# Talking-heads attention in a decoder kernel: a written order on every engine, and an entry's steps over six ticks

## The chip, the cores and the metric

The kernel runs on one core of a Trainium2 chip. The core has four engines that compute, each with an instruction queue of its own that is worked off in order: PE (TensorE, matrix products), DVE (VectorE), ACT (ScalarE) and POOL (GpSimd). SP (SyncE) issues most of the transfers (DMAs) between the chip's main memory and the on-chip memory. The metric is the device time of one execution in microseconds (us); lower is better. The times of before are a median of three executions, and one more execution was recorded by the hardware profiler.

## What is computed

The reference is a decoder of four blocks of attention, cross attention and feed-forward on x of 32 entries x 128 tokens x 128 features. The change lies in one stage, the talking-heads attention of the last block (`_L3_attn_ref`), here cut to what matters, for 16 heads of 64 features:

```python
q, k, v = (x @ Wq, x @ Wk, x @ Wv)                  # split into heads; 4 memory columns go ahead of k and v
q, k = l2norm(q), l2norm(k)
dots = einsum('bhid,bhjd->bhij', q, k) * 10.0       # 128 x 132 for each head
dots = einsum('hg,bgij->bhij', W_pre_th, dots)      # mix the heads
dots = where(causal, -max, dots)
vk = top_k(dots, 64)[0][..., -1:]                   # the 64th largest of each row
attn = softmax(where(dots < vk, -max, dots))
attn = einsum('hg,bgij->bhij', W_post_th, attn)     # mix the heads again
out = einsum('bhij,bhjd->bhid', attn, v) * head_scale_params
out = out * sigmoid(x @ Wg + bg)
return out @ Wo
```

x here is the layer-normed input, and the result is added to x.

## The kernel before, in words

The kernel runs the twelve layers one after the other, each as a stage of its own. The stage in question is `l3_attn` of class `Fast` (from line 2079). Its loop goes over ticks; each tick calls seven functions, each for another of the 32 entries, so that the steps of one entry are spread over five ticks: `queries` at lag 0, `dots` and `mixed` at lag 1, `ranked` and `kept` at lag 2, `spread` (with `gates` for every second entry) at lag 3, `outputs` at lag 4. `normed` prepares four entries at a time.

One entry goes this way:

- `queries`: PE multiplies x by the weights of q and k (into the pool p2); ACT squares each half (tile sq) and copies it (tile raw); DVE sums the squares (ss, line 2173) and makes the first guess of the reciprocal root (`rsqrt`, lines 1784 and 1785); POOL refines it in twelve small operations (lines 1787 to 1791) and scales raw (line 2176).
- `dots`: PE transposes raw (line 2188), ACT copies the transposes to qT and kT, PE multiplies them head by head (dp), ACT copies the products (tile dots, line 2197). SP writes them to main memory in 16 DMAs (scr, line 2204) and reads them back in one, with head and row inside the partition (tile rows, line 2207).
- `mixed`: PE mixes the heads and adds the causal mask (mp); ACT makes the exponentials (ex, line 2224) and a plain copy (e2, line 2225; the profile calls it e); POOL subtracts a middle part of e2 from a mask (neg, line 2228), so that the same instructions can find smallest values there.
- `ranked`: DVE searches the 64th largest value of each row. The rows stand in 16 blocks `ib` of 8 query positions; blocks 0 to 6 need no search. A round is MAX8 (the eight largest) and MATCH_REPLACE8 (strike them out), which comes with a MATCH_VALUE_LOAD. Blocks 14 and 15 are searched in e2 with eight MAX8 each (lines 2241 and 2243), blocks 7 to 13 in neg with one to seven (lines 2253 and 2255). Lines 2258 and 2259 pick the thresholds (sel, thr).
- `kept`: DVE strikes out what is under the threshold and sums the rest (line 2270, an operation of two inputs, with an accumulator read), and takes reciprocals (den, line 2272); POOL multiplies ex by them in eight operations (line 2277). The `with` at line 2273 puts these behind the neg of the next entry on POOL.
- `spread`: PE mixes again (am for the four memory columns, tp for the rest); ACT copies (am, aT); POOL spreads am over a block-diagonal tile (aM, line 2289); PE and ACT make v.
- `outputs`: PE multiplies by v (op), DVE multiplies by the gates (o, line 2330), PE projects (y), DVE adds to X (`addx`, line 387) and takes the statistics of the next norm (lines 360 and 361).

All matrix products that are issued through a helper carry line 355 in the profile; the tile's name tells them apart. Two kinds of on-chip accumulator banks are used by all steps: p2 (two buffers) and p1 (four).

What sets the order: in this stage the framework's scheduler is free. It takes all instructions, with their dependencies, and lays each engine's queue by priority and by its own estimate of durations; the order of the text is only where it begins. Two other stages (`stream` and `l3_ffn`) use the class `Ordered` (line 1347) instead: it wraps each engine in a `Lane` (line 1329), which ties every instruction to the one traced before it on that engine, so that the queue follows the text. DMAs issued by SP are not in a lane.

Of the kernel before, what the change touches and what calls it, by code (L numbers as in the profile page):

```python
# [1358 lines left out]
class Fast(General):  # L1359
# [417 lines left out]
    def rsqrt(self, wk, v, name, eng=None):  # L1777

        nc, n = self.nc, v.shape[-1]
        eng = eng or nc.vector  # L1780
        y = wk.tile([128, n], F32, tag="ry" + name, name="ry")
        t = wk.tile([128, n], F32, tag="rt" + name, name="rt")
        yi = y.bitcast(I32)
        nc.vector.tensor_scalar(yi, v.bitcast(I32), 1, None, ALU.logical_shift_right)
        nc.vector.tensor_scalar(yi, yi, -1.0, 1597463007.0, ALU.mult, ALU.add)
        for _ in range(3):
            eng.tensor_tensor(t, y, y, ALU.mult)
            if eng is nc.gpsimd:
                eng.tensor_tensor(t, t, v, ALU.mult)
                eng.tensor_scalar(t, t, -0.5, 1.5, ALU.mult, ALU.add)  # L1790
                eng.tensor_tensor(y, t, y, ALU.mult)
            else:
                eng.scalar_tensor_tensor(t, t, -0.5, v, ALU.mult, ALU.mult)
                eng.scalar_tensor_tensor(y, t, 1.5, y, ALU.add, ALU.mult)
        return y
# [283 lines left out]
    def l3_attn(self):  # L2079
        if self.general:  # L2080
            return super().l3_attn()
        nc, tc, i = self.nc, self.tc, self.i
        J, WID, AT, PAT = 132, self.WID, self.AT, self.PAT
        with ExitStack() as es:
# [77 lines left out]
            def queries(n):  # L2162
                x = X[n // 4][:, 128 * (n % 4):128 * (n % 4) + 128]
                raw = wk.tile([128, 32, 64], F32, tag="raw", name="raw")
                ss = wk.tile([128, 32], F32, tag="ss", name="ss")
                for w in range(2):
                    pp = self.p2([128, 16, 64], "qk")
                    for u in range(2):
                        self.mm(pp[:, 8 * u:8 * u + 8, :], x, aw[:, w, 512 * u:512 * u + 512])
                    sq = wk.tile([128, 16, 64], F32, tag="sq", name="sq")  # L2170
                    nc.scalar.activation(sq, pp, AF.Square)
                    nc.scalar.copy(raw[:, 16 * w:16 * w + 16, :], pp)
                    nc.vector.tensor_reduce(ss[:, 16 * w:16 * w + 16], sq, AX.X, ALU.add)
                nc.vector.tensor_scalar(ss, ss, 1e-24, None, ALU.max)
                rn = self.rsqrt(wk, ss, "s", nc.gpsimd)
                nc.gpsimd.tensor_tensor(raw, raw, rn.unsqueeze(2).to_broadcast([128, 32, 64]), ALU.mult)
                S[n] = {"raw": raw}

            def dots(n):
                flat = S[n]["raw"].rearrange("p h d -> p (h d)")  # L2180
                qT = wk.tile([128, 8, 128], F32, tag="qT", name="qT", bufs=1)
                kT = kT2[n % 2]
                for w, dst in ((0, qT), (1, kT[:, :, 4:J])):
                    for u in range(2):
                        p = self.p1([128, 4, 128])
                        for c in range(4):
                            o = 1024 * w + 512 * u + 128 * c
                            nc.tensor.transpose(p[:, c, :], flat[:, o:o + 128], self.ident)
                        nc.scalar.copy(dst[:, 4 * u:4 * u + 4, :], p)
                d = wk.tile([128, 8, 2, J], F32, tag="dots", name="dots", bufs=1)  # L2190
# [19 lines left out]
            def mixed(n):  # L2210
# [4 lines left out]
                for u, parts in enumerate((((0, 0, 416), (416, 0, 400)), ((816, 0, 264), (1080, 0, 264)))):  # L2215
                    p = self.p2([128, 2, 512], "mp")
                    for v, (at, _, m) in enumerate(parts):
                        w = 416 if u == 0 else 264
                        h = (416 * v if u == 0 else 832 + 264 * v)
                        self.mm(p[:, v, 0:w], self.identh[:, 0, :], hide[:, h:h + w], stop=False)  # L2220
                        self.mm(p[:, v, 0:m], mix1, rows[:, at:at + m], start=False)
                    w = 416 if u == 0 else 264
                    dst = slice(0, 832) if u == 0 else slice(832, 1360)
                    nc.scalar.activation(ex[:, dst].rearrange("p (v j) -> p v j", v=2), p[:, :, 0:w], AF.Exp)
                    nc.scalar.copy(e2[:, dst].rearrange("p (v j) -> p v j", v=2), p[:, :, 0:w])

                neg = wk.tile([128, 748], F32, tag="neg", name="neg")
                turn = nc.gpsimd.tensor_tensor(neg, hide2, e2[:, 348:1096], ALU.subtract)
                s.update(e2=e2, ex=ex, neg=neg, turn=turn)

            def ranked(n):

                s = S[n]
                t16 = t16_2[n % 2]
                top = wk.tile([128, 2, 8], F32, tag="top", name="top")
                thr = wk.tile([128, 7], F32, tag="thr", name="thr")
                for ib in (14, 15):
                    cur = seg(s["e2"], ib, 0, 8 * ib + 12)
                    work = wk.tile([128, J], F32, tag="work", name="work", bufs=1)
                    for r in range(8):  # L2240
                        nc.vector.max(top[:, ib - 14, :], cur)
                        if r < 7:
                            nc.vector.match_replace(out=work[:, 0:8 * ib + 12], in_to_replace=top[:, ib - 14, :],  # L2243
                                                    in_values=cur, imm_value=-3.4e38)
                            cur = work[:, 0:8 * ib + 12]
                for ib in range(7, 14):
# [13 lines left out]
                s.update(thr=thr, top=top)  # L2260

            def kept(n):
# [10 lines left out]
                with tc.issue_after(S[n + 1]["turn"].ins) if n + 1 < NB else ExitStack():  # L2273
                    for q in range(4):
                        for o, lo, m in ((exm2[n % 2][:, 4 * q:4 * q + 4, 0:4], 0, 4),
                                         (four(ex, q, 4, WID[q] - 4), 4, WID[q] - 4)):
                            nc.gpsimd.tensor_tensor(o, four(ex, q, lo, m),
                                                    d[:, 4 * q:4 * q + 4].unsqueeze(2).to_broadcast([128, 4, m]), ALU.mult)

            def spread(n):  # L2280
# [7 lines left out]
                aM = wk.tile([128, 16, 16, 8], F32, tag="aM", name="aM", bufs=1)  # L2288
# [8 lines left out]
                v = wk.tile([128, 1024], F32, tag="v", name="v")  # L2297
# [5 lines left out]
                s.update(aM=aM, v=v)  # L2303
# [15 lines left out]
            def outputs(n):  # L2319
                s = S.pop(n)  # L2320
# [8 lines left out]
                o = wk.tile([128, 8, 128], F32, tag="o", name="o", bufs=1)  # L2329
                nc.vector.scalar_tensor_tensor(o, T[n // 2][:, :, 128 * (n % 2):128 * (n % 2) + 128], 1.0, op,  # L2330
                                               ALU.add, ALU.mult)
                y = self.p1([128, 128], "y")
                for c in range(8):
                    self.mm(y, o[:, c, :], awo[:, c, :], start=c == 0, stop=c == 7)
                self.addx(n, y)

            T = {}
            normed(0)
            for t in range(NB + 5):
                if t % 4 == 3 and t + 1 < NB:  # L2340
                    normed((t + 1) // 4)
                for fn, lag in ((dots, 1), (queries, 0), (outputs, 4), (spread, 3), (ranked, 2), (mixed, 1), (kept, 2)):
                    n = t - lag
                    if 0 <= n < NB:
                        if fn is spread and n % 2 == 0:
                            gates(n // 2)
                        fn(n)
            self.look(den)

# [567 lines left out]
```

## Time and profile before

| | us |
|---|---|
| median of three executions | 6465.49 (6462.71 to 6470.9) |
| the profiled execution's own time | 6466.63 |
| its span, first to last instruction | 6464.7 |
| busy in the span: PE / DVE / POOL / ACT | 5634.8 / 4862.1 / 3699.6 / 3286.9 |
| first matmul of the stage on its weights (tile aw) | starts at 1855.5 |
| first and last neg (entries 0 and 31) | 1901.4 and 2810.0 |
| last addition to X in the stage | starts at 2850.36 |

The profile gives busy time per engine, groups of instructions by line, engine and tile with their mean durations and the idle time before them, what each wait ended on, and the instructions in order of time. In such lines `out<-in` are the tiles written and read, followed by partitions x elements. A duration runs from an instruction's start to its end, and on DVE two independent instructions may overlap a little: the start of the next one, not the end of the last, tells how long an instruction holds its engine. The times within the profile count from the start of the span.

### The profile page before, as it was taken

Reading aid. Unit: us, or ns where it says so; the run is one execution under the profiler, and the core shown is the slowest. Engines: PE = TensorE matmul, PEld = TensorE weight load, DVE = VectorE, ACT = ScalarE, POOL = GpSimd, SP = SyncE. Lnnn points to the kernel's source line nnn. Section 1 sums busy time; section 2 is a strip of 40 time slices with the busy share of each in tenths; the row PEclk is TensorE's granted clock in tenths of the full one; section 3 lists DMA queues with packets and bytes.
Section 4 is the critical chain, followed back from the end, with each engine's and each line's share of the span. In section 5 each row is a group of like instructions: output and inputs, shape, how many; then the busy total and the mean of one; then the engine's idle time right before and its main releaser. Section 6 shows DMA issues by size and latency. Waiting matters only on the chain.

```text
span 6464.7 us, 137972 instructions
## 1 busy us (share of the span) xinstructions
PE 5634.8 (87%) x56460; PEld 3993.0 (62%) x56705; DVE 4862.1 (75%) x11852; ACT 3286.9 (51%) x4413; POOL 3699.6 (57%) x4504
## 2 busy tenths in 40 slices
PE   7955966776868888876999999999999999999998
PEld 4533546664556666664676666667767666766765
DVE  4566533335549998866889988989998998998985
ACT  4645631113535555532556655665655665566554
POOL 0031001011015555523888888888888888888885
PEclk9977977668989999987999999999999999999999
DMA  1000037543002121210000000000000000000000
GB/s 40 2 1 1 2 143 237 176 138 98 8 20 51 46 50 45 51 32 34 1 1 1 14 5 1 14 5 1 1 14 5 1 14 5 1 1 1 1 1 15
DMA packets 243267, 207.49 MB, mean 32 GB/s; under 512 B 125651, under 2 KB 230458, under 8 KB 237503
## 3 DMA queue, kind: packets, MB, share of 16 engines
q1 hardware_dynamic: 239020, 161.73, 8.7%
q0 software_dynamic: 2304, 33.56, 1.4%
q8 instruction: 448, 7.34, 0.5%
q10 hardware_dynamic: 1298, 3.26, 0.1%
q14 instruction: 197, 1.61, 0.1%
HBM read 140.57 MB, written 57.93 MB: 31 GB/s over the span
## 4 chain that ended last, share of the span: by engine, by line
PE 51%; DVE 16%; POOL 2%; ACT 2%; issue 2%; DMA 0%; POOLq 0%; DVEq 0%; ACTq 0%
PE qk L1342 9%; PE sc L1342 6%; PE av L1342 6%; PE y L1342 5%; PE rT L1342 4%; PE vp L1342 4%; DVE raw L1342 2%; PE ap L1342 2%; PE gp L1342 2%; PE fy L1342 2%; PE oTp L1342 2%; PE y L355 2%; DVE ry L1342 2%; DVE work L2243 1%; PE tp L355 1%
## 5 line engine op out<-in xcount | busy, mean ns | idle before, releaser
L1342 POOL TENSOR_TENSOR raw<-raw,rt 128x1024 f32<-128x1024 f32 x384 | 1035.2, 2709 | 37.4 <-DVE raw L1342 37.4
L1342 POOL TENSOR_TENSOR raw<-raw,ry 128x2048 f32<-128x2048 f32 x192 | 741.4, 3861 | 15.0
L1342 PE MATMUL qk<-wqkv,zs 128*128 128x512 f32 x1536 | 730.0, 598 | 6.3 <-DVE zs L1342 6.3
L1342 DVE TENSOR_TENSOR raw<-qk,tab 128x1024 f32<-128x1024 f32 x384 | 700.3, 1824 | 1.3
L1342 ACT COPY qk<-qk 128x1024 f32<-128x1024 f32 x384 | 388.7, 1012 | 398.9 <-PE qk L1342 398.9
L1342 DVE TENSOR_TENSOR rt<-qk,tab 128x1024 f32<-128x1024 f32 x384 | 499.1, 1300 | 103.9 <-POOL ry L1342 44.4
L1342 PE MATMUL rT<-ident,raw 128*128 128x128 f32 x3072 | 431.2, 279 | 86.4 <-DVE qkT L1342 59.6
L1342 PEld LDWEIGHTS rT<-ident,raw 128*128 128x128 f32 x3072 | 345.3, 142 | 233.1 <-issue 99.8
L1342 ACT COPY va<-vp 128x1024 f32<-128x1024 f32 (+1 forms) x232 | 218.4, 942 | 506.6 <-PE vp L1342 505.2
L1342 DVE TENSOR_REDUCE ss<-sq 128x16 f32<-128x1024 f32 x384 | 462.8, 1205 | 0.0
L1342 ACT ACTIVATE PT<-sc 128x1024 f32<-128x1024 f32 x384 | 372.7, 1025 | 168.9 <-PE sc L1342 168.4
L1342 ACT ACTIVATE sq<-qk 128x1024 f32<-128x1024 f32 x384 | 407.9, 1062 | 75.3 <-DVE ss L1342 67.5
L1342 PEld LDWEIGHTS y<-wo,oT 128*128 128x128 f32 x3072 | 372.9, 192 | 91.1 <-issue 89.3
L1342 PEld LDWEIGHTS sc<-qkT 64*128 64x128 f32 x6144 | 359.0, 188 | 81.8 <-issue 81.8
L1342 PE MATMUL av<-va,P 128*64 128x65 f32 x12288 | 400.7, 223 | 0.0
L1342 ACT ACTIVATE P<-sc 128x1024 f32<-128x1024 f32 x384 | 372.5, 1022 | 51.3 <-PE sc L1342 50.2
L1342 PE MATMUL sc<-qkT 64*128 64x128 f32 x6144 | 395.8, 279 | 0.0
L1342 PEld LDWEIGHTS av<-va,P 128*64 128x64 f32 x12288 | 374.1, 137 | 23.8 <-issue 0.8
L1342 PEld LDWEIGHTS qk<-wqkv,zs 128*128 128x128 f32 x1536 | 264.9, 192 | 196.7 <-issue 189.1
L1342 POOL TENSOR_TENSOR X<-X,brep 128x512 f32<-128x512 f32 x24 | 30.5, 1272 | 617.8 <-DVE xn L1342 617.8
L1342 PE MATMUL y<-wo,oT 128*128 128x128 f32 x3072 | 374.3, 275 | 0.8 <-DVE qkT L1342 0.8
L1342 PE MATMUL vp<-wqkv,zs 128*128 128x512 f32 x768 | 361.6, 593 | 0.0
(438 smaller groups left out, 13099.8 us busy)
## 6 DMA issues: line engine op xcount, KB each, us to landing
rows<-scr SPq DMA_DIRECT2D x32, 672.0 KB
tup<-whole SPq DMA_DIRECT2D x8, 2048.0 KB
gt<-tup SPq DMA_DIRECT2D x64, 256.0 KB
tdn<-whole SPq DMA_DIRECT2D x8, 2048.0 KB
gd<-tdn SPq DMA_DIRECT2D x128, 128.0 KB
T<-flt SPq DMA_DIRECT2D x16, 1024.0 KB
wqkv<-in_dqkv SPq DMA_DIRECT2D x6, 1536.0 KB
scr<-dots SPq DMA_DIRECT2D x128, 66.0 KB
```

Of the source, the lines that this page charges most:

```text
L355: self.nc.tensor.matmul(out, lhsT=lhsT, rhs=rhs, start=start, stop=stop)
L1342: self.last = call(*a, **k)
L2243: nc.vector.match_replace(out=work[:, 0:8 * ib + 12], in_to_replace=top[:, ib - 14, :], in_values=cur, imm_value=-3.4e38)
```

## The change

`l3_attn` now runs under `Ordered`: on PE, DVE, ACT and POOL every instruction keeps the place that the text gives it. The functions are cut into smaller ones so that the text can be laid out: `queries` is called for q and for k separately, `summed` takes the sums and the guess, `scaled` POOL's part, `turned` the transposes; `ranked` becomes `ranked_above` (blocks 14 and 15) and `ranked_below` (7 to 13), their loops unchanged; neg moves to `negated`, POOL's multiplications by den to `divided` (the four small ones now ahead of the four large), v and the gates to `valued`; `outputs` becomes `weighted`, `gated`, `outputs` and `added`. `rsqrt` gets its first guess from a function `guess` of its own, with the same two instructions. The explicit tie of line 2273 goes. The lags grow by one behind `mixed`: an entry now takes six ticks. `normed` comes at the end of its tick, not at the start. No instruction is added or left out.

```diff
-    def rsqrt(self, wk, v, name, eng=None):
...
+    def guess(self, wk, v, name):
+        nc = self.nc
+        y = wk.tile([128, v.shape[-1]], F32, tag="ry" + name, name="ry")
         yi = y.bitcast(I32)
         nc.vector.tensor_scalar(yi, v.bitcast(I32), 1, None, ALU.logical_shift_right)
         nc.vector.tensor_scalar(yi, yi, -1.0, 1597463007.0, ALU.mult, ALU.add)
+        return y
+
+    def rsqrt(self, wk, v, name, eng=None, y=None):
...
+        y = self.guess(wk, v, name) if y is None else y
...
     def l3_attn(self):
...
-        nc, tc, i = self.nc, self.tc, self.i
+        tc, i, plain = self.tc, self.i, self.nc
+        nc = self.nc = Ordered(plain, tc)
...
-            def queries(n):
+            def queries(n, w):
...
+                pp = self.p2([128, 16, 64], "qk")
+                for u in range(2):
+                    self.mm(pp[:, 8 * u:8 * u + 8, :], x, aw[:, w, 512 * u:512 * u + 512])
+                sq = wk.tile([128, 16, 64], F32, tag="sq", name="sq")
+                nc.scalar.activation(sq, pp, AF.Square)
+                nc.scalar.copy(S[n]["raw"][:, 16 * w:16 * w + 16, :], pp)
+                S[n]["sq"].append(sq)
+
+            def summed(n):
+                ss = S[n]["ss"]
+                for w, sq in enumerate(S[n]["sq"]):
                     nc.vector.tensor_reduce(ss[:, 16 * w:16 * w + 16], sq, AX.X, ALU.add)
                 nc.vector.tensor_scalar(ss, ss, 1e-24, None, ALU.max)
-                rn = self.rsqrt(wk, ss, "s", nc.gpsimd)
+                S[n]["y0"] = self.guess(wk, ss, "s")
+
+            def scaled(n):
+                raw = S[n]["raw"]
+                rn = self.rsqrt(wk, S[n]["ss"], "s", nc.gpsimd, S[n]["y0"])
                 nc.gpsimd.tensor_tensor(raw, raw, rn.unsqueeze(2).to_broadcast([128, 32, 64]), ALU.mult)
...
-                neg = wk.tile([128, 748], F32, tag="neg", name="neg")
-                turn = nc.gpsimd.tensor_tensor(neg, hide2, e2[:, 348:1096], ALU.subtract)
...
+            def negated(n):
+
+                neg = S[n]["neg"] = wk.tile([128, 748], F32, tag="neg", name="neg")
+                nc.gpsimd.tensor_tensor(neg, hide2, S[n]["e2"][:, 348:1096], ALU.subtract)
...
+            def ranked_above(n):
                 s = S[n]
...
                 for ib in (14, 15):
...
+            def ranked_below(n):
+                s = S[n]
...
                 for ib in range(7, 14):
...
-                with tc.issue_after(S[n + 1]["turn"].ins) if n + 1 < NB else ExitStack():
-                    for q in range(4):
...
+            def divided(n):
+                ex, d = S[n]["ex"], den[:, n, :]
+                parts = [(exm2[n % 2][:, 4 * q:4 * q + 4, 0:4], q, 0, 4) for q in range(4)]
+                parts += [(four(ex, q, 4, WID[q] - 4), q, 4, WID[q] - 4) for q in range(4)]
+                for o, q, lo, m in parts:
+                    nc.gpsimd.tensor_tensor(o, four(ex, q, lo, m),
+                                            d[:, 4 * q:4 * q + 4].unsqueeze(2).to_broadcast([128, 4, m]), ALU.mult)
...
+            steps = ((ranked_above, 3), (mixed, 2), (weighted, 5), (gated, 5), (ranked_below, 3), (scaled, 1), (turned, 1),
+                     (queries, 0, 0), (dots, 1), (kept, 3), (divided, 4), (spread, 4), (negated, 2), (outputs, 5),
+                     (queries, 0, 1), (summed, 0), (added, 5), (valued, 4))
             for t in range(NB + 5):
+                for fn, lag, *a in steps:
+                    if 0 <= t - lag < NB:
+                        fn(t - lag, *a)
                 if t % 4 == 3 and t + 1 < NB:
                     normed((t + 1) // 4)
-                for fn, lag in ((dots, 1), (queries, 0), (outputs, 4), (spread, 3), (ranked, 2), (mixed, 1), (kept, 2)):
-                    n = t - lag
-                    if 0 <= n < NB:
-                        if fn is spread and n % 2 == 0:
-                            gates(n // 2)
-                        fn(n)
             self.look(den)
+        self.nc = plain
```

The pairs in `steps` are a function and its lag; a third number is the half that `queries` makes.

## The prediction

> **What bounds the kernel now.** I read the page's slices first (VectorE, the DVE row, is at 8 to 9 tenths from slice 11 to 17), then found the stage by its tiles: the first matmul on aw starts at 1855.5 us, the last write of X by line 387 ends at 2850.65. The subtractions into neg, one per entry, run from 1901.4 to 2810.0: 31 steps, 29.31 us each. The table of stretches gives the shares inside the stage (columns: stretch, length, then busy us of PE, PEld, DVE, ACT, POOL).
>
> ```profile
> core 0: us, PE busy (x) PEld busy (x) DVE busy (x) ACT busy (x) POOL busy (x), PEclk, DMA share, GB/s
> 2300.00:2700.00 400.00, 345.52 (x2628) 259.28 (x2626) 358.62 (x1970) 215.32 (x343) 207.95 (x302) 0.96 0.19 46
> ```
>
> 400 us hold 13.65 entries. Per entry DVE is busy 26.3 us of 29.3, PE 25.3, ACT 15.8, POOL 15.2. DVE is the bound, PE close behind. The groups of DVE by form say that not all of DVE's time is work.
>
> ```profile
> L2241 DVE MAX8 top<-work 128x8 f32<-128x132 f32 x91 | 25.9, 284 | 0.0
> L2258 DVE TENSOR_TENSOR sel<-t,pick 128x112 f32<-128x112 f32 x14 | 9.8, 698 | 0.4
> L2270 DVE SCALAR_TENSOR_TENSOR ex<-e,top,ex 128x132 f32<-128x132 f32 x14 | 14.5, 1036 | 0.0
> L2270 DVE SCALAR_TENSOR_TENSOR ex<-e,thr,ex 128x68 f32<-128x68 f32 x14 | 10.2, 729 | 0.4
> ```
>
> The third row has a median of 340 ns and a longest of 3623: now and then it stands still as long as a POOL operation (aM takes 3722). With the 124-wide sister (873 against 323) the excess per entry is 0.70 + 0.55 + 0.46 + 0.44 = 2.15 us. MAX8 shows none. So DVE's real work is 26.3 - 2.15 = **24.1 us**; 2.15 are stalls beside POOL, 3.0 idle. The waits in the same stretch (total us, times, longest) name most of that idle time:
>
> ```profile
> DVE top L2241 <- ACT e L2225: 15.1, 13, 1.2
> DVE t L2253 <- POOL neg L2228: 10.0, 13, 0.8
> ```
>
> The first is 1.1 us per entry: ranking waits for e2 of the same tick; the second is 0.73.
>
> Last I looked at how the ranking runs. Columns: start, duration, instruction. First a stretch of two independent blocks in turn, then the end of the last block, alone.
>
> ```profile
> 2827.36 0.45 DVE L2253 MAX8 t<-neg 128x8 f32<-128x116 f32 x2
> 2827.72 0.08 DVE L2255 MATCH_VALUE_LOAD neg<-t,neg 128x8 f32 x1
> 2827.78 0.27 DVE L2255 MATCH_REPLACE8 neg<-t,neg 128x116 f32<-128x116 f32 x1
> 2827.96 0.09 DVE L2255 MATCH_VALUE_LOAD neg<-t,neg 128x8 f32 x1
> 2828.03 0.26 DVE L2255 MATCH_REPLACE8 neg<-t,neg 128x108 f32<-128x108 f32 x1
> 2828.20 0.45 DVE L2253 MAX8 t<-neg 128x8 f32<-128x116 f32 x2
> ```
>
> ```profile
> 2831.20 0.09 DVE L2255 MATCH_VALUE_LOAD neg<-t,neg 128x8 f32 x1
> 2831.28 0.27 DVE L2255 MATCH_REPLACE8 neg<-t,neg 128x116 f32<-128x116 f32 x1
> 2831.58 0.28 DVE L2253 MAX8 t<-neg 128x8 f32<-128x116 f32 x1
> 2831.90 0.27 DVE L2258 TENSOR_TENSOR sel<-t,pick 128x112 f32<-128x112 f32 x1
> 2832.20 0.27 DVE L2259 TENSOR_REDUCE thr<-sel 128x7 f32<-128x112 f32 x1
> ```
>
> In the first, two rounds (MAX8, load, replace) take 0.84 us, 0.42 each, because the next instruction starts before the previous ends: the replace of 0.27 is followed after 0.18. In the second each instruction needs the one before, and starts 0.30 to 0.32 after it, its duration plus 0.03 to 0.04. **A dependent start costs 0.12 us more than an independent one** (0.30 - 0.18; for 132 columns 0.284 + 0.035 - 0.20 = 0.12; for 76 columns 0.22 + 0.035 - 0.14 = 0.115).
>
> **The change, part by part.** Nothing is added or removed in work; only neg's POOL edge goes, and the queues of PE, DVE, ACT and POOL now follow the text. SP's 17 DMAs per entry stay; no DMA is issued elsewhere in the loop.
>
> *DVE.* Before, the scheduler was free to mix blocks; the trace shows blocks of ib 14 and 15 running in turn with those of 7 to 13. Now ranked_above and ranked_below are written block by block, round by round, so MAX8, load, replace, MAX8 is one dependent chain. Rounds with a replace per entry: 2 x 7 above, 0+1+...+6 = 21 below, 35 in all. Each has two dependent starts (load after MAX8, MAX8 after replace; the load hides 0.06 before its replace in both orders). 35 x 2 x 0.12 = 8.4 us. Nine more chains are written end to end (sel, thr, first kept, reciprocal, maximum of ss, two of the guess, two of added): 9 x 0.11 = 1.0 us. Against this the stalls (2.15) and waits go: the two-input operations stand in kept, after ranking. The tick of DVE becomes 24.1 + 8.4 + 1.0 = **33.5 us**. Replace to MAX8 is in the trace; MAX8 followed at once by its own load is not. Its price lies between 0 (the load starts as after a stranger, then the tick is 33.5 - 35 x 0.12 = 29.3) and 0.15 (one gap more than sel shows; 34.6). I take 0.12 by the nearest row, sel after MAX8, 0.32 for a duration of 0.28.
>
> The Trainium skill, page "VectorE: DVE Perf Modes", section "The DRAIN you can't avoid", holds against this: after every operation the next waits until the pipe is empty, and leaving out semaphores between chained copies saves nothing. By that, dependent order would be free, DVE's tick 24.1 and the time that of the faster rival below. The rows above disagree (0.18 against 0.30), and I go by them.
>
> *POOL.* Per tick from 2502 to 2525: small rsqrt steps 3.9, raw 3.6, divided 3.5, aM 3.7, neg 1.8, 16.5 us. Counting from the start of ranked_above, scaled begins at -0.7 (its guess is done before added and normed), raw ends at 6.9, divided at 10.4; aM waits for PE's am behind dots (about 14) and ends near 18, neg near 20. kept starts at 10.1 + 1.1 + 15.3 = 26.5: cover of 6 us; if it goes, kept stalls as now, up to 2.15 us.
>
> *PE and ACT.* mixed 2.7 and weighted 3.6 stand first, turned after raw (6.9), queries, dots; am and tp to about 18, y, queries, v, gates to 24 (29 with gates). gated on DVE comes at 10.1 and needs weighted, done by about 3.5 to 7: cover of 3 us or more. Behind a late gated stand ranked_below and all of DVE; PE's dots too, if they need op's bank (two banks of that pool). summed comes at 29.4, its sq is there near 24; added comes at 32, y near 20. All these cost nothing while DVE's tick is 33.5.
>
> *Loop through the DMAs.* turned(n), queries, dots(n), rows(n), mixed(n), weighted, turned(n+1) are now a closed chain in PE's order. PE's parts: 1.75 + 1.85 + 2.6 + 2.7 + 3.6, plus a last copy of 0.7. The DMA leg:
>
> ```profile
> 2553.90 8.28 SPq L2204 DMA_DIRECT2D scr<-dots  x16
> 2564.73 0.34 SPq L2207 DMA_DIRECT2D rows<-scr  x1
> ```
>
> DMA traffic ceases at 2568.5, so the leg takes at least 14.6 us; for the first entry mixed started 7.4 after the issue, so at most 18.3. The loop is 27.8 to 31.5: under 33.5, but no faster than today's 29.3 by more than 1.5.
>
> *Sum.* 31 steps of 33.5 against 29.31: +130. Ticks 3, 4 lack gated and added (1.8 each), ticks 32, 33 lack summed (2.9 each), a little of it eaten by the loop: -8. Fill: ranking of entry 0 now stands behind summed(2), whose queries stand behind mixed(0), which waits for rows (1894 to 1897); 1897 + mixed 1.5, turned 1.9, queries and dots 7, sq 1, reduce and guess 1.9 is 1910, against 1901.4: +9. Drain: from ranking of entry 31, 29.4 + the 15.5 that today's tail takes after the reciprocal (2835.5 to 2851.2), against 41.2: +4. Sum +135. The profiled execution took 6466.63 us (span 6464.7 and 1.9 around it), the median is 1.1 less: 6601.8 and 6600.6. I say **6601**.
>
> **Rivals.**
>
> *Faster: dependent starts are free.* If a chain costs DVE nothing, its tick is 24.1, and PE, 25.3 busy, sets a tick near 26: 31 x -3.3 + 13 = -89, 6376. For it: DVE's 5.1 us of stalls and waits do go. Against: the 0.30 rows, and the DMA loop of at least 27.8. Break-even with today is a tick near 28.9, or 0.05 per dependent start instead of 0.12. Chance 0.04.
>
> *Half the price.* MAX8 to load costs nothing: DVE's tick is 29.3, and the DMA loop (27.8 to 31.5, middle 29.7) decides: 31 x 0.4 + 13 = +25, about 6490. Chance 0.07.
>
> *In-order queues wait for each other.* Dots are held by op's bank until gated (11.2), then go singly through one bank (+3), and rows, mixed and weighted miss the next gated. The slack on that path is about 5 us for an ordinary tick; the tick with gates and normed has less. Ticks of 34.7 to 36.5: 6640 to 6695. For: 16 instructions in four queues share two banks. Against: each order above has slack. Chance 0.07.
>
> *The order isn't kept, DVE still mixes blocks.* Then stalls go and waits stay, 6450 to 6480, in the middle 6465. Against: every instruction traced in the stage is tied to its predecessor. Chance 0.02.
>
> **How the numbers follow.** Forecast 0.80: its own span is the price of a dependent start, 0.11 to 0.13 (1.6 us per tick, 50 us), so 6576 to 6626, and ends 10 us uncertain. The range 6560 to 6640 adds the near edge of the queue rival and leaves out the half price and the faster cases. A measurement can tell 0.2%, 12.9 us, from no change. Slower: 0.80 + 0.07 + 0.07 = 0.94, less 0.02 for a half price that falls inside 0.2%: 0.92. Faster 0.04 + 0.01, same 0.02 + 0.01.
>
> **What would show it.** Right: one entry every 33 to 34 us, DVE above 95% busy or waiting only on itself; MAX8 of block 15 starting 0.30 to 0.32 after the replace before it and loads 0.3 after their MAX8; the form ex<-e,top,ex 128x132 at 340 ns with no 3.6 us case; POOL idle while kept runs. Wrong: loads 0.2 after their MAX8; DVE waiting for PE op or PE y every tick; PE waiting for rows at mixed and late at turned.

## The result, and the profile after

| | before | after |
|---|---|---|
| median of the compared executions, us | 6468.19 (6462.71 to 6473.0) | 6625.66 (6620.1 to 6648.61) |
| ratio, with its 95% interval | 1 | 1.025 (1.0225 to 1.0276) |
| span of the profiled execution, us | 6464.7 | 6621.9 |
| start of the last entry's addition to X, us | 2850.36 | 3012.69 |

The changed kernel is slower by 2.5%, 157.5 us by the medians. The end of the stage moved by 162.3 us; what comes after the stage takes 5.1 us less, which makes the 157.2 us of the spans. So all of it is in this stage.

The table of stretches of the kernel after, for the same 400 us as before (columns: stretch, length, then busy us of PE, PEld, DVE, ACT, POOL, the granted clock, DMA share, GB/s):

```profile
2300.00:2700.00 400.00, 306.53 (x2251) 223.62 (x2250) 367.13 (x1719) 183.36 (x293) 177.86 (x268) 0.91 0.18 42
```

DVE is busy for more of the time than before (367.1 against 358.6) and starts fewer instructions (1719 against 1970). PE, ACT and POOL all do less in the same time. An engine that is busier and gets less done has longer instructions, or instructions that overlap less. The groups by form tell which (in the last two columns: total us and mean ns of one, then idle us before them):

```profile
L1342 DVE MAX8 top<-work 128x8 f32<-128x132 f32 x77 | 23.0, 299 | 2.7
...
L1342 DVE SCALAR_TENSOR_TENSOR ex<-e,top,ex 128x132 f32<-128x132 f32 x12 | 4.2, 352 | 0.0
L1342 DVE SCALAR_TENSOR_TENSOR ex<-e,thr,ex 128x68 f32<-128x68 f32 x12 | 3.4, 280 | 0.0
L1342 DVE TENSOR_TENSOR sel<-t,pick 128x112 f32<-128x112 f32 x12 | 3.3, 274 | 0.4
```

The two-input operations, which took 1036, 729 and 698 ns before, take 352, 280 and 274: the stalls beside POOL are gone. MAX8 itself went from 284 to 299. The time is between the instructions. Here are two rounds of block 14 of the kernel after, in order of time (start, duration):

```profile
2526.29 0.29 DVE L1342 MAX8 top<-work 128x8 f32<-128x124 f32 x1
2526.61 0.09 DVE L1342 MATCH_VALUE_LOAD work<-top,work 128x8 f32 x1
2526.69 0.27 DVE L1342 MATCH_REPLACE8 work<-top,work 128x124 f32<-128x124 f32 x1
2526.99 0.29 DVE L1342 MAX8 top<-work 128x8 f32<-128x124 f32 x1
2527.32 0.09 DVE L1342 MATCH_VALUE_LOAD work<-top,work 128x8 f32 x1
```

Read the first column. From MAX8 to its load 0.32 to 0.33 us, from the replace to the next MAX8 0.30: each starts when the one before has ended, and 0.03 later. A round takes 0.70 to 0.71 us (0.725 with 132 columns, 0.695 with 116). Before, two rounds in turn took 0.84 in the rows with 116 and 108 columns.

The waits in the same stretch (total us, times, longest) show that no other engine holds DVE up; the only one of DVE's with a place in the list is the last row, and PE waits for the DMAs but has room for it:

```profile
POOL rt L1342 <- DVE ry L1342: 139.3, 12, 12.5
...
PE mp L1342 <- DMA rows<-scr: 31.4, 9, 6.1
...
DVE xnT L1342 <- PE p L1342: 1.7, 3, 0.6
```

On the chips of the experiments below the kernel before itself took between 6448 and 6668 us (once 18040), and in six of the profiles (runs 4 to 7, 9 and 10) the part behind the stage takes 3699 to 3795 us instead of the 3609 to 3642 of the others; therefore the experiments are read mainly by lengths inside the stage, beside the program's times, whose medians take slow executions in and whose ratios leave them out.

### The profile page after: what moved, and what is told of

The parts are those of the page before. It is cut to its first block, busy times and chain, and to the rows that moved or that the text cites. A ratio compares the mean times of both kernels' runs of the same rounds, so it can differ in the third digit from the quotient of the medians.

```text
span 6621.9 us, 138235 instructions
## 1 busy us (share of the span) xinstructions
PE 5682.8 (86%) x56705; PEld 4000.9 (60%) x56705; DVE 5017.2 (76%) x11852; ACT 3282.7 (50%) x4413; POOL 3699.5 (56%) x4504
## 5 line engine op out<-in xcount | busy, mean ns | idle before, releaser
L1342 POOL TENSOR_TENSOR raw<-raw,ry 128x2048 f32<-128x2048 f32 x224 | 857.5, 3828 | 17.6
L1342 POOL TENSOR_TENSOR rt<-ry 128x32 f32<-128x32 f32 (+1 forms) x816 | 235.3, 288 | 633.5 <-DVE ry L1342 526.8
L1342 ACT ACTIVATE sq<-qk 128x1024 f32<-128x1024 f32 x448 | 473.3, 1057 | 202.8 <-PE qk L1342 125.7
L1342 DVE TENSOR_REDUCE ss<-sq 128x16 f32<-128x1024 f32 x448 | 536.5, 1203 | 48.4 <-ACT sq L1342 48.4
L1342 POOL TENSOR_SCALAR rt<-rt 128x32 f32<-128x32 f32 (+1 forms) x816 | 343.6, 421 | 71.4
```

The source lines that it names most:

```text
L1342: self.last = call(*a, **k)
```

## The experiments

*Theory:* the ranking, written block after block, is one chain of dependent instructions, and that is the loss; a second limit, the loop through the DMAs, stands close under it. *Rivals:* the order of the engines' queues as such costs the time (they wait for each other); or DVE's order as a whole does, of which the ranking is only a part.

The table has all runs. A tick is the distance from the first neg to the last one, over 31; the stage runs from its first matmul on aw to its last of y. The column of DVE splits DVE's time per entry into ranking, other work and waits. It is counted in the traces from the start of one instruction to the start of the next, from the sel of entry 4 to that of entry 28; a wait is a gap of more than 0.15 us. The three add up to a little more than the tick, because the first and last ticks, which the tick's mean includes, are shorter.

| run | what it is | tick | stage | DVE: ranking / other / waits | program, median (lowest) | ratio to before, 95% |
|---|---|---|---|---|---|---|
| | before | 29.31 | 994.6 | 16.8 / 10.1 / 2.8 | 6468.2 (6462.7) | 1 |
| | after | 33.66 | 1159.8 | 25.6 / 8.6 / 0.1 | 6625.7 (6620.1) | 1.0225 to 1.0276 |
| 1 | after, ranking in turn | 30.80 | 1056.2 | 17.1 / 9.6 / 4.2 | 6532.4 (6528.2) | 1.0009 to 1.0160 |
| 2 | before, ranking block by block | 33.80 | 1150.4 | 24.4 / 8.8 / 1.2 | 6626.0 (6618.7) | 1.0126 to 1.0313 |
| 3 | run 1, mixing moved | 29.00 | 1001.9 | 17.1 / 11.0 / 1.6 | 6492.9 (6469.5) | 0.9907 to 1.0104 |
| 4 | after, DVE's order left to the scheduler | 35.22 | 1179.5 | 20.5 / 13.8 / 1.7 | 6787.1 (6733.4) | 1.0285 to 1.0603 |
| 5 | run 1, another order of the steps | 29.92 | 1026.8 | 17.0 / 9.6 / 4.3 | 6510.3 (6488.7) | 1.0016 to 1.0084 |
| 6 | after, mixing moved | 34.55 | 1187.6 | 25.6 / 9.5 / 0.1 | 6702.8 (6654.0) | 1.0257 to 1.0410 |
| 7 | run 5, ranking block after block | 39.04 | 1326.1 | 25.6 / 10.5 / 4.5 | 6861.7 (6790.5) | 1.0484 to 1.0650 |
| 8 | run 5, gates ahead of y, norm split | 28.71 | 988.6 | 17.0 / 11.7 / 0.5 | 6566.9 (6488.3) | 0.9949 to 1.0264 |
| 9 | after, only blocks 14 and 15 in turn | 31.52 | 1086.7 | 22.0 / 8.6 / 1.2 | 6645.6 (6616.7) | 1.0054 to 1.0369 |
| 10 | run 8, guess and norm ahead of kept | 28.07 | 967.5 | 17.0 / 8.7 / 2.7 | 6569.0 (6420.8) | 0.9797 to 1.0052 |
| 11 | run 10, gating behind blocks 14 and 15 | 26.33 | 912.4 | 17.0 / 8.6 / 0.9 | 6382.8 (6371.5) | 0.9856 to 0.9894 |

From before to after the ranking takes 8.8 us more of DVE's time, other work 1.5 less and waits 2.7 less; that makes the 4.6 us by which an entry became longer. The ranking takes 25.6 us wherever its blocks stand one after the other in a written queue (after, runs 6 and 7) and 17.0 to 17.1 wherever they stand in turn (runs 1, 3, 5, 8, 10 and 11). Counted one by one, 71 starts an entry in the ranking of the kernel after (70, and that of sel) come only when the instruction before has ended, in the mean 302 ns behind its start, and the others after 180 ns: a dependent start costs 0.12 us more. In turn, six of the 71 are left.

### Run 1: the chain undone, all else as after

```diff
-                for ib in (14, 15):
...
-                    for r in range(8):
-                        nc.vector.max(top[:, ib - 14, :], cur)
...
+                for r in range(8):
+                    for ib in (14, 15):
+                        nc.vector.max(top[:, ib - 14, :], cur[ib])
+                    for ib in (14, 15):
+                        if r < 7:
+                            nc.vector.match_replace(out=work[ib], in_to_replace=top[:, ib - 14, :], in_values=cur[ib],
+                                                    imm_value=-3.4e38)
...
+                for pair in zip(rounds((13, 11, 8)), rounds((12, 10, 9, 7))):
+                    for t8, cur, _ in pair:
+                        nc.vector.max(t8, cur)
+                    for t8, cur, more in pair:
+                        if more:
+                            nc.vector.match_replace(out=cur, in_to_replace=t8, in_values=cur, imm_value=-3.4e38)
```

`rounds` lists a group of blocks round by round; blocks 13, 11 and 8 go in turn with 12, 10, 9 and 7. The instructions are the same ones; the tile `work` gets a second buffer, so that two blocks can be struck out side by side.

> The changed kernel with one thing undone: DVE no longer runs one block of the ranking after the other; blocks 14 and 15 go in turn, and blocks 13, 11, 8 in turn with 12, 10, 9, 7, so that a stranger always stands between two dependent instructions. Every queue stays in written order. Theory (the price is the dependent chain, about 0.13 us per dependent start, 70 starts): DVE's tick falls from 33.75 to about 24.7, and then the loop through the DMAs sets the tick, 29.8 by the changed kernel's trace (turned at 2499.78, the end of the next weighted at 2529.6); 31 x (29.8 - 34) = -130, so 6485 to 6510. Rival (the in-order queues wait for each other whatever DVE's chain costs): the tick stays at 33 or more, 6600 to 6625.

Measured: the stage is 104 us shorter (1159.8 to 1056.2), the tick falls from 33.66 to 30.80, a little above what was expected, and the program's 6528 is 18 us above the expected span. The order of the ranking in DVE's own queue, with nothing else changed but that buffer, is worth 104 of the 165 us that the change added to the stage. What holds the tick now is named by the waits of this run:

```profile
DVE o L1342 <- PE op L1342: 48.5, 12, 6.0
...
PEld mp L1342 <- DMA rows<-scr: 42.3, 13, 6.6
```

DVE waits for op, 12 times in 13 entries, and PE waits for rows every time: the loop turned, queries, dots, rows, mixed, weighted, turned is closed, at 30.8 us. The prediction had put it at 27.8 to 31.5. Of the 8.5 us that the ranking gives back, DVE now waits 4.1 and works 1.0 longer beside POOL (sel takes 528 ns, the first operation of kept 1027).

### Run 2: the chain alone, in the kernel before

```diff
+                tied = Lane(nc.vector, tc)
...
-                        nc.vector.max(top[:, ib - 14, :], cur)
+                        tied.max(top[:, ib - 14, :], cur)
...
-                            nc.vector.match_replace(out=work[:, 0:8 * ib + 12], in_to_replace=top[:, ib - 14, :],
+                            tied.match_replace(out=work[:, 0:8 * ib + 12], in_to_replace=top[:, ib - 14, :],
```

The same for the loop of blocks 7 to 13: each ranking instruction is tied to the ranking instruction before it; the scheduler is free with everything else.

> The kernel of before with one thing done alone: the ranking instructions of an entry are tied to each other in the order of the text, everything else is left to the scheduler as it was. Theory: the dependent starts cost up to 70 x 0.13 = 9 us per entry, of which the scheduler hides a part by putting DVE's other 25 instructions or so into the gaps (3 at most), and the stalls beside POOL stay: 35 to 38 us per entry, 6650 to 6740. Rival: the chain costs little and the changed kernel's loss is in its queues: within 20 us of before, 6450 to 6490.

Measured: the tick rises by 4.5 us to 33.80, the stage by 156 us, the program to 6626, as with the whole change. The loss was expected to be larger (35 to 38 us, 6650 to 6740): tied so, the scheduler puts other work into the gaps (ranking 24.4 us, not 25.6), and the stalls of the two-input operations go here too for the greater part (sel 274 ns; three of the forms in kept still have means of 425 to 677 ns). The rival, for which the ranking's order is worth at most 20 us, falls. A written order on the other engines is not needed for the loss.

### Runs 3 and 6: the DMA loop opened, with and without the chain

```diff
-            steps = ((ranked_above, 3), (mixed, 2), (weighted, 5), (gated, 5), (ranked_below, 3), (scaled, 1), (turned, 1),
-                     (queries, 0, 0), (dots, 1), (kept, 3), (divided, 4), (spread, 4), (negated, 2), (outputs, 5),
-                     (queries, 0, 1), (summed, 0), (added, 5), (valued, 4))
+            steps = ((ranked_above, 3), (weighted, 5), (gated, 5), (ranked_below, 3), (scaled, 1), (turned, 1),
+                     (queries, 0, 0), (dots, 1), (kept, 3), (divided, 4), (spread, 4), (outputs, 5),
+                     (queries, 0, 1), (mixed, 2), (negated, 2), (summed, 0), (added, 5), (valued, 4))
```

Run 3 is this on top of run 1, run 6 is this alone on the kernel after.

> The kernel with the blocks in turn, and one step moved: mixed stands behind the second queries, negated behind it, so that PE no longer has mixed, which waits for rows, ahead of weighted and turned. Theory (with the chain gone, the loop through the DMAs is the bound of the kernel with blocks in turn): the loop is opened, and the next one is summed, scaled on POOL (7.5), turned, queries, dots, am and tp, y, queries, sq, summed: 27 us by the changed kernel's trace (2525.03 to about 2552); PE with gates needs 27.8 every second tick. The tick becomes 27 to 28.5: 6410 to 6460, faster than both. Rival (the rows do not bind there): no difference from the kernel with blocks in turn, within 10 us.

> The changed kernel with its ranking block after block as it is, and only mixed and negated moved behind the second queries. Theory (the chain on DVE is the bound and the waits of PE for rows cost nothing there): no gain, 33.5 to 34.5 per entry, 6605 to 6630. Rival (those waits, 69 us in 400, are part of the loss): a gain of 30 us or more, 6590 or less.

Measured: with the chain gone, PE no longer waits for rows and the tick falls by 1.8 us to 29.00, 0.5 above the expected span; the program's lowest time, 6469.5, is 10 us above it. With the chain in place the tick does not fall: as long as DVE sets the tick, a wait of PE is worth nothing. It even rises (34.55 against 33.66), and the program's lowest time, 6654, is above the expected 6605 to 6630: the ranking takes the same 25.6 us, but neg now runs while DVE is at kept, whose two-input operations take 0.9 us more. (The 69 us of waits in that expectation count the same nine waits of PE twice, once for the weights and once for the product.) In run 3 something else stands in the way, seen in the groups by form:

```profile
L1342 DVE TENSOR_TENSOR sel<-t,pick 128x112 f32<-128x112 f32 x14 | 23.6, 1685 | 0.5
...
L1342 DVE SCALAR_TENSOR_TENSOR ex<-e,thr,ex 128x108 f32<-128x108 f32 x13 | 7.7, 591 | 0.0
```

sel takes 1685 ns instead of 274: DVE reaches it sooner, and POOL's aM still runs. In this order of the steps the stalls that the change had removed come back when the ranking is short: the cover was there only because DVE was late.

### Run 4: DVE without a lane

```diff
+        nc.vector = plain.vector
```

PE, ACT and POOL keep the written order, the scheduler lays DVE's queue.

> The changed kernel with DVE left to the scheduler; PE, ACT and POOL keep the written order. Theory: the scheduler mixes the blocks of the ranking again, DVE's dependent starts vanish from the path, and the loop through the DMAs sets the tick near 30: 6480 to 6530. Rival (the queues of PE, ACT and POOL cost the time): the tick stays at 33 or more, 6600 or above.

The expectation failed: the tick is 35.22, not near 30, and by its numbers it is the rival that came. The trace says why. Blocks 14 and 15 stand in a chain again, with nothing of 7 to 13 between them (from 2523.61 on, a round takes 0.71 us, as after); DVE then waits for neg, 18.2 us in 400, which comes late on POOL's written queue. That this is why the scheduler had nothing to mix in is a reading of the trace and was not tried by itself. Blocks 7 to 13, behind neg, do stand in turn, mostly two at a time, but for the end of block 13:

```profile
2507.09 0.25 DVE L2278 MATCH_REPLACE8 neg<-t,neg 128x108 f32<-128x108 f32 x1
2507.26 0.08 DVE L2278 MATCH_VALUE_LOAD neg<-t,neg 128x8 f32 x1
2507.33 0.25 DVE L2278 MATCH_REPLACE8 neg<-t,neg 128x100 f32<-128x100 f32 x1
2507.49 0.43 DVE L2276 MAX8 t<-neg 128x8 f32<-128x108 f32 x2
```

So the ranking takes 20.5 us an entry, 5.1 less than after, and yet the entry is longer. What takes the gain away stands beside POOL: sel, next to raw, and kept, next to the divisions.

```profile
2514.51 3.62 POOL L1342 TENSOR_TENSOR raw<-raw,ry 128x2048 f32<-128x2048 f32 x1
2515.48 2.78 DVE L2281 TENSOR_TENSOR sel<-t,pick 128x112 f32<-128x112 f32 x1
```

```profile
L2281 DVE TENSOR_TENSOR sel<-t,pick 128x112 f32<-128x112 f32 x12 | 38.5, 3208 | 0.4
```

Against after, sel takes 2.9 us an entry more and kept another 2.9, and the wait for neg is new. A scheduler on one engine beside written queues on the others undid only part of the chain and lost more at another place; this run alone does not separate theory from rival. Runs 1 and 2 do.

### Run 9: part of the chain

The edit is the upper half of run 1's: blocks 14 and 15 in turn, 7 to 13 as after.

> The changed kernel with only blocks 14 and 15 in turn (14 of the 35 rounds), blocks 7 to 13 one after the other as they are. Theory: 14 rounds x 0.27 us = 3.8 us leave DVE's tick, 34.0 - 3.8 = 30.2, and the DMA loop of 30.8 takes over: the gain is nearly all of what the kernel with all blocks in turn had: 6525 to 6550. Rival (the gain comes in proportion to the rounds put in turn, 40%): 6575 to 6595.

Measured: 1086.7 us of stage, 73 of the 104 us of run 1, with 14 of the 35 rounds undone; a tick of 31.52. A tick in strict proportion to the rounds would be 33.66 - 0.4 x 2.86 = 32.5, and the whole price of a pair (14 x 0.27 = 3.8 us) would give 29.9. It lies between them; the program's lowest time, 6616.7, is above the spans of both theory and rival. DVE's column says where the gain went: the ranking is 3.6 us shorter, nearly the 3.8 that were expected, and 1.1 of it comes back as a wait for op. PE waits for rows here too (39.6 us in 400, for 10 entries), so the loop takes part of the gain.

### Runs 5 and 7: another order of the steps, with and without the chain

```diff
+            steps = ((weighted, 5), (gated, 5), (divided, 4), (spread, 4), (ranked_above, 3), (ranked_below, 3),
+                     (queries, 0, 0), (queries, 0, 1), (mixed, 2), (scaled, 1), (turned, 1), (negated, 2), (dots, 1),
+                     (kept, 3), (outputs, 5), (summed, 0), (added, 5), (valued, 4))
```

Run 5 has this and the pairs of run 1; run 7 has this with the blocks one after the other.

> Blocks of the ranking in turn, and another written order: PE begins the tick with weighted, then am and tp, both queries, mixed, turned, dots; DVE begins with gated, so that op's bank is free early; POOL begins with divided and aM, then scaled and neg, so that it is done when DVE comes to sel and kept. Theory (what is left after the chain is the DMA loop, and after it the stalls beside POOL: in the kernel with mixed moved, sel took 1685 ns instead of 274): both are gone, DVE needs 24.1 + 1 + half a microsecond for normed, PE 26.3 with every second tick longer; 26.5 to 27.5 per entry, 31 x -2.3 + 15 = -56, so 6395 to 6430. Rival (a further loop through the two banks of p2 or through POOL holds the tick): 28.5 to 30 per entry, 6450 to 6510.

> The second written order (POOL first with divided and aM, DVE first with gated), but the ranking block after block as in the changed kernel. Theory: the chain costs its 0.13 us at 70 places here too, DVE's tick is 33.5 to 34.2, 6600 to 6630, and the difference to the same order with blocks in turn is 6 to 8 us per entry, 190 to 230 us. Rival (the order of the steps decides, not the order inside the ranking): within 60 us of the kernel with blocks in turn.

Measured: 29.92 in turn, 39.04 in a chain, in the same order of steps: 9.1 us an entry, more than the 6 to 8 expected. The ranking makes 8.6 of it (25.6 against 17.0), about 0.12 us for each of its 70 dependent starts, and here all of that shows; 0.9 more is the guess of the roots, which stands beside POOL in run 7 (ry<-ry 1219 ns in the mean against 181). Against the order of after (33.66 to 30.80), where the loop took over at 30.8, only 2.9 could be seen. Run 7's own tick was expected at 33.5 to 34.2: the 4.5 us an entry that DVE waits there, as in run 5 (4.3), were left out. Run 5 did not reach its expected tick either, its rival's span (28.5 to 30) came, for a reason that its waits name:

```profile
DVE o L1342 <- PE op L1342: 51.7, 10, 6.0
...
PE gp L1342 <- DVE X L1342: 19.3, 7, 3.1
```

Every second entry, the last matmul of the gates wants the bank of y, which DVE gives back in `added`, behind kept; PE stands, and op is late for the next tick. In run 7 the same wait grew to 58.8 us.

### Runs 8, 10 and 11: what is left when the chain is gone

Run 8 puts v and the gates ahead of y, and cuts `normed` in three (centred on DVE, flipped on PE, copied on DVE). Run 10 moves DVE's guess and the centring ahead of kept. Run 11 moves the gating behind blocks 14 and 15. The final order:

```diff
+            steps = ((weighted, 5), (divided, 4), (spread, 4), (ranked_above, 3), (gated, 5), (ranked_below, 3),
+                     (queries, 0, 0), (queries, 0, 1), (summed, 0), (centred,), (mixed, 2), (scaled, 1), (turned, 1),
+                     (negated, 2), (dots, 1), (kept, 3), (valued, 4), (flipped,), (outputs, 5), (copied,),
+                     (added, 5))
```

> The second written order with blocks in turn, and its one remaining wait taken away: in its trace every second tick the last matmul of the gates waits for the accumulator bank that y holds until DVE's addition at the end of the tick (2.5 us), and weighted behind it makes gated on DVE wait 6.0 us. Now v and the gates stand ahead of y, and normed is cut in three (centred early on DVE, its transposes behind the gates, its copy ahead of the addition). Theory: both waits vanish; a tick without gates stays at 25.5 us, one with gates at 27 to 28: 26.3 to 27 per entry, 31 x -2.6 + 15 = -65, so 6385 to 6420, faster than before and than the changed kernel. Rival (the bank was only the first of several waits): 29 or more, 6450 or above.

> This is the second other order again (ranking blocks in turn, gates ahead of y, the norm split) with DVE's guess of the roots and its four centring operations put directly behind the ranking and ahead of the kept entries. In the run before, they stood behind the kept entries, where POOL is multiplying aM, and one of them took up to 3.6 us; behind the ranking POOL is done with the divisions and with aM. Theory (small TENSOR_SCALARs of DVE stall only beside a running POOL operation): ry<-ry falls from 1.9 us to about 0.2 in the mean, DVE's tick falls by 2 to 3 us from 28.7, that is to 25.5 to 27; PE, with about 26.3 us of work per entry, becomes the bound or close to it; the stage takes 910 to 940 us, the program 6385 to 6430 us, 0.6 to 1.2% under the kernel before. Rival (the long TENSOR_SCALARs wait for something of DVE's own, the kept entries ahead of them or the table of the gates): they stay at over 1 us wherever they stand and the tick stays at 28 to 29, the program within 0.4% of the kernel before.

> The third other order, with one step moved on DVE: the gating product o<-th,op of entry t-5 stands behind the ranking of blocks 14 and 15 instead of ahead of it, so that DVE ranks while PE still makes op. In the run before, DVE waited 28.5 us in 400 (2.0 us an entry) for op at that place, and POOL, ACT and PE waited behind DVE's kept entries in turn (POOL exm <- DVE den 10.6 us an entry). Theory (the tick of 28.1 is DVE's 24.9 us of work plus this wait and some gaps): the wait goes, the tick falls to 25.5 to 26.8, where PE's own work stands; the stage takes 890 to 935 us instead of 967.5, the program 6360 to 6410 us in its fastest runs. Rival (op's bank, held 8 us longer, makes PE wait for DVE ahead of the queries or of the mixing, as the bank of y did in the first other order): PE waits for DVE o at qk or mp, the tick stays at 28 or rises, and the stage takes 965 us or more.

Run 8: PE's waits for the bank of y went, but the tick was 28.71 instead of 26.3 to 27, and the program's lowest time 6488 instead of 6385 to 6420. DVE's operations of the guess, 182 ns each in the kernel after, had become long. Its group by form, and in order of time one of them beside POOL's aM:

```profile
L1342 DVE TENSOR_SCALAR ry<-ry 128x32 int32<-128x32 int32 x14 | 26.8, 1912 | 0.5
```

```profile
2462.52 3.72 POOL L1342 TENSOR_TENSOR aM<-am,own 128x2048 f32<-128x2048 f32 x1
2462.63 3.64 DVE L1342 TENSOR_SCALAR ry<-ry 128x32 int32<-128x32 int32 x1
```

It begins 0.11 us behind aM and ends with it, for 32 elements a partition.

Run 10: moved to where POOL is idle, the same operations take 182 ns, so that theory held; the tick fell less than expected (28.07), because DVE stands at the head of its tick for op:

```profile
L1342 DVE TENSOR_SCALAR ry<-ry 128x32 int32<-128x32 int32 x14 | 2.5, 182 | 0.5
```

```profile
DVE o L1342 <- PE op L1342: 28.5, 10, 3.5
```

Run 11: the wait for op is gone, the tick is 26.33, the stage 912.4 us, all within the expected spans, and the program at 6382.8 us is 1.25% under the kernel before (1.06% to 1.44%). The rival (PE waits for op's bank) shows in the waits with only 5.6 us in 400, at qk. Its table of stretches and, in order of time, its ranking:

```profile
2300.00:2700.00 400.00, 369.39 (x2929) 273.71 (x2927) 375.47 (x2213) 234.44 (x375) 235.00 (x353) 1.00 0.22 54
```

```profile
2514.68 0.48 DVE L1342 MAX8 top<-work 128x8 f32<-128x124 f32 x2
2515.08 0.07 DVE L1342 MATCH_VALUE_LOAD work<-top,work 128x8 f32 x1
2515.14 0.27 DVE L1342 MATCH_REPLACE8 work<-top,work 128x124 f32<-128x124 f32 x1
2515.33 0.08 DVE L1342 MATCH_VALUE_LOAD work<-top,work 128x8 f32 x1
2515.39 0.28 DVE L1342 MATCH_REPLACE8 work<-top,work 128x132 f32<-128x132 f32 x1
2515.59 0.28 DVE L1342 MAX8 top<-work 128x8 f32<-128x124 f32 x1
```

Two rounds, one of either block, in 0.91 us where the kernel after takes 0.71 + 0.725. Both DVE and PE are now busy for over 92% of the stretch, and 400 us hold 15.2 entries instead of 11.9. A written order, then, can beat the scheduler's here. That of the change does not, even with its ranking in turn (run 1: a tick of 30.80 against 29.31): it took the ranking in turn and another order of the steps.

## Why the prediction was right

The forecast was 6601 and the range 6560 to 6640; the kernel takes 6625.7, and the forecast case is the one that came. Step by step:

- **The price of a dependent start.** Forecast 0.12 us more than an independent one, MAX8 to its own load included, which the trace of before did not show. Measured: that pair takes 0.32 to 0.33 us in the kernel after against 0.20 for a start in turn (run 11: two MAX8 of 0.28 stand together in 0.48). In the mean a dependent start takes 302 ns and another 180, 0.12 us less; from before to after the ranking grew by 8.8 us where 8.4 was forecast. The value was chosen by the nearest row, and the row carried.
- **The tick.** Forecast 33.5. Ordinary ticks take 33.75, each fourth one, with the norm, 36.05: 34.33 in the mean. Most of the 0.8 that are missing lie in the base and not in the price: 24.1 was DVE's busy time of 26.3 less 2.15 of stalls, but counted from start to start, with the short gaps, DVE's work before was 26.9 (16.8 + 10.1). From 26.9 - 2.15 = 24.7 the 9.4 of the forecast lead to 34.1; measured are 34.2 of work and 0.1 of waits. Over the steady part, entry 0 to entry 31: forecast 31 x 33.5 - 8 = 1030, measured 1053.0, so +144 against 908.6 before, where +122 was said. This is the largest miss of the sum.
- **The stalls go.** Right: 352 ns with no long case, POOL idle while kept runs. Runs 3 and 4 show what that cover is worth: when DVE comes to sel while POOL works, 1.4 and 2.9 us an entry return at sel alone. The cover hangs on the order of the steps: in runs 5, 8, 10 and 11 sel takes 275 ns with a ranking as short as in run 3.
- **The loop through the DMAs.** Forecast 27.8 to 31.5, under DVE's tick. Runs 1, 3 and 6 confirm it: 30.8 when the chain is gone, 29.0 when the loop is opened too, and no gain from opening it while the chain stands.
- **Fill.** The ranking of entry 0 was put at 1910 and starts at 1910.17: +8.8 for +9.
- **Drain.** Forecast +4, measured +9.2 (2963.15, the ranking of entry 31, to 3012.69, against 2810.0 to 2850.36). From the reciprocal to the last addition to X the tail was taken over from before (15.5 in the prediction; the trace has 15.06 from start to start); it takes 19.55. In the written order y of entry 30 (1.95 us) and v of entry 31 (1.88, and ACT's copy of it, 1.0) stand in PE's queue ahead of the last op, and the products tp, which come after 6.9 us without work for PE, take 5.96 us at a granted clock of 0.63 (2994 to 3001) where they took 4.01 at 1.00 (2838 to 2843 before); the first product of the tail starts 1.7 us sooner. The step that failed is that the tail would stay as it was: in a written queue, the drain has the whole order of a tick in it.
- **The sum.** +8.8 +144.4 +9.2 = 162.4 at the end of the stage, 5.1 less behind it: 157.3. The forecast was 135.

The Trainium skill, page "VectorE: DVE Perf Modes", section "The DRAIN you can't avoid", says that the next operation does not start until the pipe is empty, and from this the prediction took the case in which order is free of charge. The same section says that an operation which is not held starts earlier, which the prediction left out; the rows in turn agree with that, and the page has no price for it. Run 1 has one: the same instructions of DVE, in turn instead of in a chain, make the stage 104 us shorter.

The rivals: "dependent starts are free" and "half the price" fall with run 2 and with runs 5 and 7. "Queues wait for each other" was not the cause in the kernel after, where DVE waits next to nothing for others (1.7 us in 400). Such waits show as soon as the chain is gone (runs 1, 5 and 10, 2.7 to 4.3 us an entry), so it names real limits, but not the one that decided. "The order isn't kept" falls with the rows of block 14 above, which stand in the order of the text.

## What to carry to other kernels

When a queue is written by hand, let independent chains take turns, round by round: a top-k search on one engine, here 70 dependent starts an entry, paid 0.12 us for each that no other work stood between. Before a written order takes a scheduler's place, look in the trace for what the scheduler had mixed, and keep that. And take the limits one at a time: here the chain, then the DMA loop, an accumulator bank, stalls beside POOL and a wait for op each hid the next, and a fix for one of them was worth nothing, or less, while the one above it stood (run 6).

## What the runs showed of the hardware

- Small one-input operations of DVE can stand as long as a POOL operation: a TENSOR_SCALAR on 128x32 elements, 0.18 us alone, took 3.64 us beside aM's 3.72 (run 8), and 182 ns in the mean where POOL was idle (run 10). MAX8 and MATCH_REPLACE8 show nothing of it: in run 11 pairs of rounds lie beside aM (2516.73 to 2520.45) and take 0.90 to 0.91 us each, as without it. Nor does X<-X,y, which has one of its two inputs in an accumulator bank: begun beside a long POOL operation it takes 271 to 291 ns (44 cases in all runs), elsewhere 280. The Trainium skill, page "SBUF — State Buffer", section "SBUF: two separate sides", speaks of an exclusive lock between POOL and a DVE operation in a two-port mode, or with two inputs there against a POOL operation that reads there. The full length of the stall agrees with a lock; this small operation has one input, and that it ran in a two-port mode no run here shows.
- sel, 128x112 elements, took 274 ns, 1685 and 3208 in the mean in three kernels with the same instruction (after, runs 3 and 4): a place beside POOL can cost more than ten times its work.
